# The fourth of four Mamba x halves convolved on VectorE, in a hybrid of convolution, attention, Mamba and a recurrence

## The chip, the cores and the metric

One core of one Trainium2 chip runs the whole program. The metric is the device time of one execution in microseconds (us): the median of several runs. Engines are called by their short names: PE is TensorE, DVE is VectorE, ACT is ScalarE, POOL is GpSimd, SP is the queue that issues most DMAs. PEld is the weight load of PE.

## The reference, cut to what matters

The input x has 4 images of 128 channels and 64 x 64 pixels. Layer 0 is a group norm, three convolutions and a non-local attention. Layer 1 takes the pixels as 4 sequences of 4096 tokens with 128 features, runs a Mamba block forward and one backward over the normalized tokens, adds both, and then runs a recurrence. The change touches the front of the two Mamba blocks alone:

```
zxbcdt = x @ in_proj
z, xbc, dt = jnp.split(zxbcdt, [D_INNER, D_INNER + CONV_DIM], axis=-1)
xp = jnp.pad(xbc, ((0, 0), (K - 1, 0), (0, 0)))
conv = sum((xp[:, i:i + l, :] * conv_w[:, i] for i in range(K))) + conv_b
xbc = jax.nn.silu(conv)
xh, Bm, Cm = jnp.split(xbc, [D_INNER, D_INNER + D_STATE], axis=-1)
...
y = _ssd(xh, dt, A, Bm, Cm) + xh * D[None, None, :, None]
yg = y.reshape(b, l, D_INNER) * jax.nn.silu(z)
```

D_INNER is 256, so xh has two halves of 128 channels in each of two directions: four halves. K is 4: the convolution is causal, along the tokens, with four taps for each channel, and is followed by a Silu. Everything is computed in float32.

## The kernel before, in words

Layer 0 fills the first half of the span, the recurrence the last tenth. Between them, from about 1,697 us on, stands the Mamba stage (function `mamba`). The features lie on the 128 partitions and the tokens run along the free axis. The stage works in **steps** of 128 tokens of each direction and in **groups** of 512 tokens, four steps to a group: 8 groups to a sequence, 32 groups in all. The loop over n (lines 1406 to 1477) takes one step per turn; j = n mod 4 is the step in the group.

A step n does, in this order on PE: `states` (L1212, the chunk's state, into `small`), `turn` for the next step (L1177, transposes of x into `ptr`), `scan` (L1234 and L1242, the outputs y), `prepare` for the next step (L1187 p_bt and L1189 p_g, into `small`). ACT does for a step the differences of decay (`lt`, L1168, eight relus), their exponential (L1191) and a copy of the transposed B (`bt`, L1193). DVE multiplies x with dt (L1196), makes `gm` (L1200), multiplies it into `lt` (L1201), and adds the new state (`S`, L1224).

Spread over the four steps is what prepares the next group and finishes the last:
- step j = 0: x projection (backward, half 0), `project_bc` for B, x projection (forward, half 1)
- step j = 1: means of the last group (L1282), x projection (backward, half 1), `project_bc` for C
- step j = 2: `project_fwd` (forward, half 0), the Silus of the three other halves (`activate`, L1139), four z projections (L1146, L1147)
- step j = 3: the output projections (`back`, L1305)

The x halves are convolved in two ways. `project` (lines 1118 to 1135) takes three of the four: PE makes one projection without taps (L1124), ACT writes bias plus the last tap times the projection (L1129, an Identity), and DVE adds the three other taps, shifted, straight from PSUM (L1135); the first columns are cleared and added from the last group (L1128, L1133). The Silu comes later, in place, in SBUF (L1139). `project_fwd` (lines 1110 to 1116) takes the fourth: the tap is multiplied into the weights beforehand (L970), so PE runs four matmuls of 128x512 that add up in PSUM (L1115), and ACT applies bias and Silu (L1116). B and C use PE's way as well (L1103, L1107).

All these projections, the z projections, the output projections and the transposes of the row statistics of other sequences (`ls_in`, L83, run at the end of a step by the generators `opening` and `ending`) share a ring of three PSUM buffers ("big", pool `m_ring`). A buffer is taken in program order and comes free when its last reader is done.

The order of instructions on PE and on ACT is written out by hand: it is the order of the calls in the loop (`manual_schedule` for these two). DVE, POOL and the DMA queues are ordered by the framework's planner. Each engine takes its instructions in order.

Of the kernel before, what the change touches and what calls it, by code (L numbers as in the profile page):

```python
# [10 lines left out]
F32 = mybir.dt.float32  # L11
AF = mybir.ActivationFunctionType
ALU = mybir.AluOpType
# [3 lines left out]
P = 128  # L17
# [9 lines left out]
DS = 64  # L27
DI = NHEAD * HD
KC = 4
GT = NC // P  # L30
DIRS = ("fwd", "bwd")
MG = 512
# [116 lines left out]
def run(parts):  # L149
    for _ in parts:  # L150
        pass
# [736 lines left out]
def mamba(nc, tc, k, a, t, B, T, vec, first=None, after=None, mr=None):  # L888
# [16 lines left out]
    with ExitStack() as ctx:  # L905
# [24 lines left out]
        wp = ctx.enter_context(tc.tile_pool(name="m_w", bufs=1))  # L930
        w = []
# [5 lines left out]
        with tc.tile_pool(name="m_ws", bufs=1) as ws, tc.tile_pool(name="m_wps", bufs=2, space=PSUM) as wps:  # L937
            full, cw = [], []
            for i, d in enumerate(DIRS):
                full.append(ws.tile([P, 2 * DI + 2 * DS + NHEAD], F32, name="full_" + d))  # L940
                nc.sync.dma_start(full[i], a[d + "_in_proj"])

                at = DI if i else 0
                cw.append(ws.tile([P, KC, DI + 2 * DS - at], F32, name="cw_" + d))
                nc.scalar.dma_start(
                    cw[i], a[d + "_conv_wt"][:, at:].unsqueeze(0).to_broadcast([P, KC, DI + 2 * DS - at])
                )
            if first is not None:
                scales(0, first)
            for i, d in enumerate(DIRS):  # L950
                centre(nc, k, wps, "c", full[i])
                nc.scalar.copy(wdt[:, bass.ts(i, NHEAD)], full[i][:, 2 * DI + 2 * DS :])
            if first is not None:
                run(scaled(0))
            for i, d in enumerate(DIRS):
                s = dict(taps=vec["taps_" + d], cb=vec["cb_" + d], D=vec["D_" + d])
                w.append(s)
                nc.gpsimd.memset(mean[:, i, i : i + 1], 1.0 / DI)
                f = full[i]
                s["z"] = wp.tile([P, DI], F32, name="wz_" + d)  # L960
                s["x"] = wp.tile([P, DI] if i else [P, KC, P], F32, name="wx_" + d)
                s["bc"] = wp.tile([P, KC, 2 * DS], F32, name="wbc_" + d)


                for c in range(KC):
                    nc.vector.tensor_tensor(
                        s["bc"][:, c, :], f[:, 2 * DI : 2 * DI + 2 * DS], cw[i][:, c, -2 * DS :], ALU.mult
                    )
                    if i == 0:
                        nc.gpsimd.tensor_tensor(s["x"][:, c, :], f[:, DI : DI + P], cw[i][:, c, 0:P], ALU.mult)  # L970
                if i:
                    nc.scalar.copy(s["x"], f[:, DI : 2 * DI])
                else:
                    s["x1"] = wp.tile([P, P], F32, name="wx1")
                    nc.scalar.copy(s["x1"], f[:, DI + P : 2 * DI])
                nc.scalar.copy(s["z"], f[:, 0:DI])
            for i, d in enumerate(DIRS):
                out = wp.tile([P, 2, P], F32, name="wout_" + d)
                w[i]["out"] = out
                nc.scalar.dma_start(out, a[d + "_out_proj"].rearrange("(c p) m -> p c m", p=P))  # L980
                for c in range(2):
                    nc.gpsimd.tensor_scalar(out[:, c, :], out[:, c, :], vec["nw_" + d][:, c : c + 1], None, ALU.mult)
# [4 lines left out]
        ring = ctx.enter_context(tc.tile_pool(name="m_ring", bufs=3, space=PSUM))  # L987
# [6 lines left out]
        def rows(g, i, c):  # L994

            return ds(g * MG + c if i == 0 else (NG - 1 - g) * MG + 2 * PAD - c, MG)
# [110 lines left out]
            act = lambda: nc.scalar.activation(gr["bc"][c], pb, AF.Silu, bias=bc_bias[:, c : c + 1])  # L1107
            act() if later is None else later.append(act)

        def project_fwd(gr):  # L1110

            tl, g = gr["tl"], gr["at"][1]
            px = ring.tile([P, MG], F32, tag="big", name="px")
            for tap in range(KC):
                nc.tensor.matmul(px, w[0]["x"][:, tap, :], tl[:, rows(g, 0, tap)], start=(tap == 0), stop=(tap == KC - 1))  # L1115
            nc.scalar.activation(gr["x"][0][:, 0, :], px, AF.Silu, bias=w[0]["cb"][:, 0:1])  # L1116

        def project(gr, i, c):


            tl, g = gr["tl"], gr["at"][1]
            px = ring.tile([P, MG], F32, tag="big", name="px")
            wx = w[1]["x"][:, bass.ts(c, P)] if i else w[0]["x1"]
            nc.tensor.matmul(px, wx, tl[:, rows(g, i, PAD)], start=True, stop=True)  # L1124
            x = gr["x+"][i][:, c, :]
            taps = w[i]["taps"][:, c, :]
            at = lambda n: x[:, PAD - n : PAD - n + MG] if i else x[:, n : n + MG]
            nc.vector.memset(x[:, 0:PAD] if i else x[:, MG:], 0.0)  # L1128
            nc.scalar.activation(at(0), px, AF.Identity, scale=taps[:, PAD:KC], bias=w[i]["cb"][:, c : c + 1])  # L1129
            if g:  # L1130
                v = x[:, MG:] if i else x[:, 0:PAD]
                past = groups[gr["at"][0] * NG + g - 1]["x+"][i][:, c, :]
                nc.vector.tensor_tensor(v, v, past[:, 0:PAD] if i else past[:, MG:], ALU.add)  # L1133
            for n in range(1, KC):
                nc.vector.scalar_tensor_tensor(at(n), px, taps[:, PAD - n : KC - n], at(n), ALU.mult, ALU.add)  # L1135
# [160 lines left out]
                m2.rearrange("q n -> (q n)").unsqueeze(0).to_broadcast([P, ND * MG]),  # L1296
            )

        STEPS_X = ((1, 0), (0, 1), (1, 1))

        def outputs(gr, d):
            po = ring.tile([P, MG], F32, tag="big", name="po")
# [47 lines left out]
        seqs, groups, m = {}, {}, {}  # L1350
# [42 lines left out]
        open_step(1)  # L1393
        for act in later:
            act()
        project_fwd(groups[0])
        for i, c in STEPS_X:
            project(groups[0], i, c)
        differences(m[0])
# [6 lines left out]
        for n in range(N):  # L1406
            G, j = divmod(n, MT)
            b, g = divmod(G, NG)
            gr = groups[G]
            last = g == NG - 1  # L1410
            if n + 2 < N:
                open_step(n + 2)
            if n % NT == 0:
                S = None
            S1 = states(m[n], S)
            if n + 1 < N:
                turn(m[n + 1])
            if n % 2 == 0:
                y = ps.tile([P, ND, 2, 2 * P], F32, tag="y", name="y")
            scan(m.pop(n), y, S)  # L1420
            S = S1
            if n + 1 < N:
                prepare(m[n + 1])
            if n % 2:
                take(gr, j, y)
            more = G + 1 < NGR
            if j == 0:
                if more:
                    open_group(G + 1)
                if G > 0:  # L1430
                    squares(groups[G - 1])
                if more:
                    project(groups[G + 1], *STEPS_X[0])
                if more:
                    project_bc(groups[G + 1], 0)
                if more:
                    project(groups[G + 1], *STEPS_X[1])
            elif j == 1:
                if G > 0:
                    means(groups[G - 1])  # L1440
                if more:
                    project(groups[G + 1], *STEPS_X[2])
                if more:
                    project_bc(groups[G + 1], 1)
            elif j == 2:
                if more:
                    project_fwd(groups[G + 1])
                if more:
                    for i, c in STEPS_X:
                        activate(groups[G + 1], i, c)  # L1450
                for i in range(ND):
                    for c in range(2):
                        project_z(gr, i, c)
                gate(gr, 1)
            elif j == 3:
                gate(gr, 3, not more)
                if not more:
                    squares(gr, (0,))
                if G > 0:
                    back(groups.pop(G - 1))  # L1460
            if n + 2 < N:
                differences(m[n + 2])

            i = n % NT
            if i == 4:
                opening = open_sequence(b + 1) if b + 1 < B else iter(())
            if i >= 4:
                run(islice(opening, 1))
            if i == 5:
                ending = ended(b - 1) if after is not None and b > 0 else iter(())  # L1470
            if i >= 5 and i % 2:
                run(islice(ending, 1))

            if mr is not None and b == B - 1 and i in (24, 25, 28, 29):
                if i == 24:
                    own = row_statistics(nc, k, ring, "big", wk, t[:, b * T :], mr, (3, 4, 2, 5, 1, 6))
                next(own)
# [276 lines left out]
```

## Time and profile before

| | |
|---|---|
| time | 3146.06 us, median of 3 (3143.19 to 3150.89) |
| span of the profiled run | 3144.2 us, granted PE clock 0.981 |
| PE busy | 2939.4 us, 93% |
| DVE busy | 2198.3 us, 70% |
| ACT busy | 1815.3 us, 58% |
| POOL busy | 1799.3 us, 57% |
| L1115, the four taps on PE | 4 matmuls of 128x512 in each of 32 groups, 256 records in the profile |
| L1124, a projection without taps | 3 in each group, 192 records |
| L1135, the multiply-adds on DVE | 288, about 749 ns each |
| L1129 and L1139 on ACT | 96 each, 778 and 619 ns (medians) |
| L1116 on ACT | 32, 687 ns, and 31 table loads of 1283 ns |

The profile writes every float32 matmul as two records of MATMUL, one behind the other; the time of one record is that of a pipelined pass, and the distance from start to start is less than it. In views that list instructions, the bracket at the end of a line tells how long the engine sat idle before it and what it waited for.

### The profile page before, as it was taken

Reading aid. Unit: us, or ns where it says so; the run is one execution under the profiler, and the core shown is the slowest. Engines: PE = TensorE matmul, PEld = TensorE weight load, DVE = VectorE, ACT = ScalarE, POOL = GpSimd, SP = SyncE. Lnnn points to the kernel's source line nnn. Section 1 sums busy time; section 2 is a strip of 40 time slices with the busy share of each in tenths; the row PEclk is TensorE's granted clock in tenths of the full one; section 3 lists DMA queues with packets and bytes.
Section 4 is the critical chain, followed back from the end, with each engine's and each line's share of the span. In section 5 each row is a group of like instructions: output and inputs, shape, how many; then the busy total and the mean of one; then the engine's idle time right before and its main releaser. Section 6 shows DMA issues by size and latency. Waiting matters only on the chain. (4 is left out here: it accounts for less than half of the span.)

```text
span 3144.2 us, 42863 instructions
## 1 busy us (share of the span) xinstructions
PE 2939.4 (93%) x15511; PEld 1459.0 (46%) x15511; DVE 2198.3 (70%) x3429; ACT 1815.3 (58%) x3102; POOL 1799.3 (57%) x1394
## 2 busy tenths in 40 slices
PE   6899999999999999999997999999999999999976
PEld 1345444454444454444453444444444445455545
DVE  7876668666777667687765767677677767676667
ACT  3343334434344433444434878787788778888756
POOL 4258448456584655766553565555555665555644
PEclk9999999999999999999998999999999999999988
DMA  5310101010100101011023333334343344333332
GB/s 182 133 40 29 38 31 45 8 43 23 46 23 30 43 23 38 31 53 34 10 77 93 93 116 93 96 95 113 84 101 92 88 112 97 96 95 98 92 109 109
DMA packets 108394, 224.16 MB, mean 71 GB/s; under 512 B 25678, under 2 KB 29390, under 8 KB 106764
## 3 DMA queue, kind: packets, MB, share of 16 engines
q1 hardware_dynamic: 96588, 177.53, 20.4%
q10 hardware_dynamic: 11584, 43.78, 4.1%
q8 instruction: 125, 2.05, 0.3%
q14 instruction: 97, 0.79, 0.1%
HBM read 200.83 MB, written 20.44 MB: 70 GB/s over the span
## 5 line engine op out<-in xcount | busy, mean ns | idle before, releaser
L477 DVE TENSOR_TENSOR es<-es,ex 128x1024 f32<-128x1024 f32 x448 | 684.2, 1527 | 137.6 <-ACT ex L462 104.5
L462 ACT ACTIVATE ex<-pf 128x1024 f32<-128x1024 f32 x512 | 497.5, 1022 | 462.3 <-PE pf L460 420.2
L460 PE MATMUL pf<-theta,phi 64*128 64x512 f32 x2048 | 513.6, 619 | 20.2 <-ACT ex L462 19.8
L471 PE MATMUL acc<-ex,gT 128*64 128x512 f32 x2048 | 490.8, 605 | 1.6 <-ACT ex L462 1.6
L1202 POOL TENSOR_TENSOR ct<-ct,Cst 128x512 f32<-128x512 f32 x128 | 171.4, 1339 | 403.2 <-DMA ct<-csmem 365.0
L460 PEld LDWEIGHTS pf<-theta,phi 64*128 64x128 f32 x2048 | 173.3, 186 | 339.4 <-ACT ex L462 173.0
L1168 ACT ACTIVATE lt<-lt,cs 128x128 f32<-128x128 f32 x1024 | 312.1, 390 | 0.5 <-DMA lt<-csmem 0.5
L367 PE MATMUL pm<-yf,wt 128*128 128x256 f32 x1152 | 287.1, 382 | 12.2 <-DVE att L483 11.0
L410 ACT ACTIVATE eo<-pm 128x256 f32<-128x256 f32 x88 | 33.8, 384 | 449.5 <-PE pm L367 443.0
L471 PEld LDWEIGHTS acc<-ex,gT 128*64 128x64 f32 x2048 | 127.4, 136 | 338.2 <-issue 326.3
L367 PEld LDWEIGHTS pm<-yf,wt 128*128 128x128 f32 x1152 | 212.9, 189 | 93.7 <-issue 39.0
L1103 PE MATMUL pb<-tl,wbc_fwd 128*64 128x512 f32 x512 | 236.2, 604 | 3.2 <-DVE xT L1135 3.2
L1103 PE MATMUL pb<-tl,wbc_bwd 128*64 128x512 f32 x512 | 236.7, 604 | 0.0
L337 POOL TENSOR_TENSOR yf<-yd 128x272 f32<-128x272 f32 x192 | 234.1, 1247 | 1.4
L1267 POOL TENSOR_TENSOR yT<-yT,zT 128x512 f32<-128x512 f32 x127 | 169.3, 1342 | 35.8 <-DVE yT L1254 32.2
L337 POOL TENSOR_TENSOR yf<-xp 128x272 f32<-128x272 f32 x128 | 109.7, 889 | 133.3 <-PE pm L367 127.5
L1201 DVE TENSOR_TENSOR lt<-lt,gm 128x1024 f32<-128x1024 f32 x128 | 180.1, 1407 | 1.9
L1135 DVE SCALAR_TENSOR_TENSOR xT<-px,taps_bwd,xT 128x512 f32<-128x512 f32 x192 | 143.7, 749 | 8.9 <-ACT xT L1129 4.0
L1234 PE MATMUL y<-lt,xdt 128*64 128x128 f32 x2048 | 142.4, 282 | 4.9 <-PE ptr L1177 4.6
L1103 PEld LDWEIGHTS pb<-tl,wbc_fwd 128*64 128x64 f32 x512 | 65.5, 138 | 164.3 <-issue 137.1
L367 PE MATMUL pm<-yf,wc 128*128 128x256 f32 x512 | 131.5, 385 | 6.6 <-DVE att L483 5.1
L414 DVE SCALAR_TENSOR_TENSOR eo<-pm,eo 128x256 f32<-128x256 f32 x176 | 72.4, 412 | 92.2 <-ACT eo L410 90.1
(297 smaller groups left out, 5694.7 us busy)
## 6 DMA issues: line engine op xcount, KB each, us to landing
lt<-csmem SPq DMA_DIRECT2D x128, 512.0 KB, 5.6
wt<-wd ACTq DMA_DIRECT2D x72, 576.0 KB, 3.8
ct<-csmem SPq DMA_DIRECT2D x256, 128.0 KB, 5.4
rs<-m SPq DMA_DIRECT2D x31, 512.0 KB, 3.9
wd<-t SPq DMA_DIRECT2D x16, 576.0 KB, 2.8
t<-in_x SPq DMA_DIRECT2D x4, 2048.0 KB, 10.8
rows<-after SPq DMA_DIRECT2D x32, 256.0 KB, 5.3
out<-t SPq DMA_DIRECT2D x4, 2048.0 KB, 14.4
```

Of the source, the lines that this page charges most:

```text
L337: nc.gpsimd.tensor_tensor(f[:, kx], at(x), at(y), op)
L367: nc.tensor.matmul(pm[:, e, :], wt, src, start=(i == 0), stop=(i == len(terms) - 1))
L460: nc.tensor.matmul(pf[:, e, :], phi[HALF[e], m, :], th[HALF[e]], start=True, stop=True)
L462: nc.scalar.activation(ex, pf, AF.Exp, scale=scale)
L471: nc.tensor.matmul(acc[HALF[e]], gT[:, 2 * m + e, :], ex[:, e, :], start=(m == 0), stop=(m == NT // 2 - 1))
L477: nc.vector.tensor_tensor(es, es, ex, ALU.add)
L1103: nc.tensor.matmul(out, w[i]["bc"][:, tap, bass.ts(c, DS)], src, start=(tap == 0), stop=(tap == KC - 1),)
L1135: nc.vector.scalar_tensor_tensor(at(n), px, taps[:, PAD - n : KC - n], at(n), ALU.mult, ALU.add)
L1168: nc.scalar.activation(v, v, AF.Relu, scale=-1.0, bias=m["b"]["cs"][:, d, m["i"], h : h + 1])
L1201: nc.vector.tensor_tensor(lt, lt, gm.unsqueeze(2).to_broadcast([P, ND, NHEAD, P]), ALU.mult)
L1202: nc.gpsimd.tensor_tensor(m["ct"], m["ct"], Cs[:, cols].unsqueeze(1).to_broadcast([P, NHEAD, P]), ALU.mult)
L1267: eng.tensor_tensor(v, v, gr["z"][d][:, :, half(d, j // 2)], ALU.mult)
```

## The change

The fourth half goes the way of the three others. `project_fwd` is gone; `project` treats all four (direction, half) pairs alike, and the list of pairs becomes ((1, 0), (0, 1), (1, 1), (0, 0)). The new projection stands at the end of step j = 1, behind `project_bc` for C, and its Silu is the last of now four in-place Silus in step j = 2. The weights multiplied by taps for this half are not made any more (four POOL products), and the broadcast of the taps that they needed gets smaller. The purpose is to take three of the four matmuls of this half off PE.

```diff
-                at = DI if i else 0
-                cw.append(ws.tile([P, KC, DI + 2 * DS - at], F32, name="cw_" + d))
+                cw.append(ws.tile([P, KC, 2 * DS], F32, name="cw_" + d))
...
-                    if i == 0:
-                        nc.gpsimd.tensor_tensor(s["x"][:, c, :], f[:, DI : DI + P], cw[i][:, c, 0:P], ALU.mult)
-                if i:
-                    nc.scalar.copy(s["x"], f[:, DI : 2 * DI])
-                else:
-                    s["x1"] = wp.tile([P, P], F32, name="wx1")
-                    nc.scalar.copy(s["x1"], f[:, DI + P : 2 * DI])
+                nc.scalar.copy(s["x"], f[:, DI : 2 * DI])
...
-        def project_fwd(gr):
-
-            tl, g = gr["tl"], gr["at"][1]
-            px = ring.tile([P, MG], F32, tag="big", name="px")
-            for tap in range(KC):
-                nc.tensor.matmul(px, w[0]["x"][:, tap, :], tl[:, rows(g, 0, tap)], start=(tap == 0), stop=(tap == KC - 1))
-            nc.scalar.activation(gr["x"][0][:, 0, :], px, AF.Silu, bias=w[0]["cb"][:, 0:1])
...
-            wx = w[1]["x"][:, bass.ts(c, P)] if i else w[0]["x1"]
+            wx = w[i]["x"][:, bass.ts(c, P)]
...
-        STEPS_X = ((1, 0), (0, 1), (1, 1))
+        STEPS_X = ((1, 0), (0, 1), (1, 1), (0, 0))
...
-        project_fwd(groups[0])
         for i, c in STEPS_X:
             project(groups[0], i, c)
...
                     project(groups[G + 1], *STEPS_X[2])
                 if more:
                     project_bc(groups[G + 1], 1)
+                if more:
+                    project(groups[G + 1], *STEPS_X[3])
             elif j == 2:
-                if more:
-                    project_fwd(groups[G + 1])
                 if more:
                     for i, c in STEPS_X:
                         activate(groups[G + 1], i, c)
```

More of the change, by code (lines that the diff above doesn't have):

```diff
@@ L941, in mamba @@
                 nc.sync.dma_start(full[i], a[d + "_in_proj"])
-                at = DI if i else 0
-                cw.append(ws.tile([P, KC, DI + 2 * DS - at], F32, name="cw_" + d))
+                cw.append(ws.tile([P, KC, 2 * DS], F32, name="cw_" + d))
                 nc.scalar.dma_start(
-                    cw[i], a[d + "_conv_wt"][:, at:].unsqueeze(0).to_broadcast([P, KC, DI + 2 * DS - at])
+                    cw[i], a[d + "_conv_wt"][:, DI:].unsqueeze(0).to_broadcast([P, KC, 2 * DS])
                 )
@@ L960, in mamba @@
                 s["z"] = wp.tile([P, DI], F32, name="wz_" + d)
-                s["x"] = wp.tile([P, DI] if i else [P, KC, P], F32, name="wx_" + d)
+                s["x"] = wp.tile([P, DI], F32, name="wx_" + d)
                 s["bc"] = wp.tile([P, KC, 2 * DS], F32, name="wbc_" + d)
```

## The prediction

> **What bounds the kernel now.** I read the table of engines first: PE is busy 93% of the span, DVE 70%, ACT 58%. The change acts only from 1,697 us on (the Mamba stage), so next I asked for the busy time from 1,738 to 2,950 us, where all but the first of its groups of 512 tokens open:
>
> ```profile
> 1738.00:2950.00 1212.00, 1158.72 (x7868) 587.93 (x7867) 854.42 (x1866) 973.47 (x1925) 698.30 (x580) 0.99 0.39 98
> ```
>
> The columns after the length are PE, PE weight loads, DVE, ACT, POOL, then the granted clock. PE is busy 96%, but ACT 80% and DVE 70%: PE leads, ACT is close behind. The chain of waits confirms PE for most of a group. A mean does not tell what ACT can take, so I read the timeline of ACT around the edited call, for the group opened at 2,340-2,356 us:
>
> ```profile
> 2344.58 0.69 ACT L1107 ACTIVATE Cst<-pb,bc_bias 128x512 f32<-128x512 f32 x1 [1.51 <-PE pb L1103]
> 2345.16 2.43 ACT L1168 ACTIVATE lt<-lt,cs 128x128 f32<-128x128 f32 x8
> 2347.61 1.28 ACT L1191 ACT_TABLE_LOAD   x1
> 2348.91 1.06 ACT L1191 ACTIVATE lt<-lt 128x1024 f32<-128x1024 f32 x1
> 2349.87 0.25 ACT L1193 COPY bt<-small 128x128 f32<-128x128 f32 x1
> 2350.14 1.28 ACT L1116 ACT_TABLE_LOAD   x1
> 2351.53 0.69 ACT L1116 ACTIVATE xT<-px,cb_fwd 128x512 f32<-128x512 f32 x1
> 2352.12 1.66 ACT L1139 ACTIVATE xT<-xT 128x512 f32<-128x512 f32 x3
> 2353.68 1.56 ACT L1147 ACTIVATE zT<-pz 128x512 f32<-128x512 f32 x3
> ```
>
> The reader is to see that ACT runs with hardly a hole from 2,344.58 to 2,355.2, while PE does as long a piece: its four taps (L1115) end just as the table load does. Two paths of equal length run from the end of the C projection (pb) to the fourth z projection. That fourth pz needs the ring slot of the first pz, which ACT frees:
>
> ```profile
> 2354.31 1.13 PE L1146 MATMUL pz<-tl,wz_bwd 128*128 128x512 f32 x2 [0.24 <-ACT zT L1147]
> ```
>
> How equal they are in each group is read from the source view of L1116, how long ACT waited for the taps:
>
> ```profile
>   PE px L1115: 30.4, 22
> ```
>
> Group by group (31 calls in the loop) the time between the end of the table load and the Silu is 0.1 us nine times, 0.34 once, 0.85 eight times, 1.2 four times, 2.06 nine times. Only where it is large is PE the longer path.
>
> **What the Trainium skill says.** "ScalarE: Activation LUTs", "What ACT_TABLE_LOAD costs" and "Table sets": a load takes 1283 ns, and identity and relu are in every set. The trace agrees: all loads are 1283 ns, and L1129 (Identity) has none. "TensorE: Matmul & The Clock Gate", Part 2, step 1: matmuls stay in program order. The trace agrees: at 2,354 us PE waits for the slot although the transposes behind it (L1177) follow at once. The same page, Part 1: after an idle window of about 3.4 us the PE clock falls to half until about 3.4 us of activity. The trace agrees on the half rate and puts the threshold lower: of PE's seven idle gaps over 2 us in the stage, five (4.22 twice, 2.86, 2.37, 2.13) are followed by slow matmuls (a px pair takes 2.07 instead of 1.13), two (2.76, 2.53) are not, and none of the gaps of 0.8-1.2 us is. After the 2.86 gap the stretch from pcs to the scan's second half takes 6.36 us, after the 2.37 gap 5.07, after the undisturbed 2.76 gap 3.50: a drop costs 1.6 to 2.9 us.
>
> **The change, part by part.**
> *PE.* Four taps of a 128x512 projection become one. They stand as 8 records at 0.43 us, 3.65 us in the chain of waits; a single projection (L1124) takes 1.06. PE alone saves 2.59 us a group, but at two places: 3.65 leave step 2, 1.06 come into step 1, right behind the C projection.
> *ACT.* Step 1 gains an Identity (L1129, 0.78 us). The same pattern stands in step 0 of this trace: Silu of B at 2,333.59, Identity of the projection behind it at 2,334.65, relu at 2,335.32, so 1.73 us from Silu to relu. In step 1 now it is 0.58. **ACT's path gets 1.15 us longer.** In step 2 a fourth in-place Silu (0.52 us from start to start) replaces one from PSUM (0.58): -0.06. The table load moves to the first in-place Silu; no load more or less.
> *DVE.* Three more multiply-adds of 0.749 us (L1135), a memset and an add of 3 columns: 2.6 us a group, 32 x 2.6 = 83 us busy. In the changed program's order on DVE they stand behind xdt and xdtd where there are no row statistics, in the 2.2-2.8 us hole in which DVE waits for ACT's bt copy: free. Where row statistics (L85) run in step 1 they stand ahead of the state update S (L1224), and PE's next p_bt (L1187) waits for S.
> *POOL, DMA, setup.* Four products of weights (L970, 4 x 0.65 us) and 512 KB of broadcast go. POOL then waits for wout's DMA anyway (2.68 us at L982), and cw has long landed: nothing.
> *Who waits.* The fourth pz is queued behind three pz on PE, and behind it all of turn, scan, po. So the time of that pz is what counts. Its shift, by class:
> - 0.1 us (9 groups): ACT is the path. 1.15 - 0.06 - 0.1 = +1.0; nine make +9.0. The one of 0.34: +0.75.
> - 0.85 (8, one row statistic): +0.24 each, +1.9. S comes about 1 us late, but the bt copy has 1.2 us of room on PE's side.
> - 1.2 (4): three -0.1; in the fourth (2,232 us) DVE lags, the slot that the row statistic takes is freed 2.3 us later: +0.9. Sum +0.6.
> - 2.06 (9): four with two row statistics: p_bt waits for S, which comes after 3 multiply-adds and 8 statistics: bt +1.4, then no wait: -0.65 each. Two with one: -0.8. Three with pcs in step 1: the new px waits for ms (L1284), bt comes 1-1.8 us later: -0.8. Sum -6.6.
> The opening group, where DVE is the chain (4.71 us of L1135 and others before the Silu): three more at 0.67, start 0.7 sooner: +1.4.
> **Sum of the paths: +7 us.**
> *The clock.* This is the unknown. PE now runs ahead and waits before the fourth pz. In the 0.1 groups: step 2 begins for PE at 2,347.8 + 1.0, three pz end at 2,351.5, the fourth starts at 2,355.3: a gap of 3.8 us instead of 0.24. In the 0.85 groups it is 2.0, in three of the 1.2 groups 2.7, in two of the 2.06 groups 2.1, else about 1.6. By the seven gaps above I take a drop as certain at 3.5 and more (10 groups), 0.7 at 2.7 and 0.5 at 2.0-2.1 (10 groups), none below. At 1.6 us, the low end since part of the slow time falls into the gap: 16 + 3.4 + 8 = 27. Bounds: 0 (no drop matters), and 31 x 2.1 = 65.
> I take the paths plus the middle of the clock's cost: 3146 + 7 + 27 = 3180, given as 3179.
>
> **The rivals.**
> 1. *PE is the bound and keeps its gain.* For it: 93% busy, PE on most of the chain. 32 x 2.59 = 83 us would give 3063; if only the groups' PE path with ACT's floor counts and ACT hides its Identity, about 1.0-1.5 a group, so 3100-3115. Against: nine groups with no wait at the Silu, where a shorter PE frees nothing. I take 3108. Faster.
> 2. *A draw.* The paths as above and no clock cost: 3153. For it: two gaps of 2.5-2.8 us passed undisturbed.
> 3. *DVE becomes the bound.* The 2.6 us fall on the state update in every group: 31 x 2.6 = 81 would give 3227; in the 17 groups with statistics or pcs, 44 us, plus the sum of the paths, 3197. For it: PE waits for S already (L1187, 34 us in 2,000-2,720). Against: DVE idles about 6 us in step 2.
>
> **How the numbers follow.** Forecast (ACT path, clock) 0.50; draw 0.25; PE's gain 0.12; DVE 0.13. Faster by over 0.3% (below 3136.6) is rival 1: 0.12. Within 0.3% (to 3155.5): 0.15 of the draw and 0.03 of the forecast: 0.18. Slower: 0.70. The range, 3141 to 3214, leaves out rival 1 and the upper part of rival 3.
>
> **What would show it.** Right: PE's wait for ACT before pz (6.8 us between 1,750 and 2,900 us now) at about 75 us; the granted clock of the stage under 0.99; relu of step 1 1.73 us after the Silu of C; ACT busy +23 us (32 x (0.78 + 0.62 - 0.69)); DVE +80; steps 2 followed by slow scans in the 0.1 groups. Wrong: if the fourth pz starts sooner than before in the 0.1 groups, or if waits for S at L1187 grow far over 60 us (rival 3), or if the gaps stand there and the scans behind them stay at 1.09 us (rival 2).

## The result, and the profile after

The changed kernel takes 3196.82 us (median; 3188.05 to 3199.23, 4 runs) against 3147.31 us (3143.19 to 3150.89; 4 runs, one more than in the table of before). The ratio is 1.0153, with a 95% interval of 1.013 to 1.0176: 1.5% slower, and 18 us above the forecast of 3179. PE does less work, and the program is longer. First, the engines of the changed kernel, from the first part of its page:

```profile
PE 2884.2 (91%) x15319; PEld 1429.8 (45%) x15319; DVE 2278.5 (72%) x3585; ACT 1838.7 (58%) x3134; POOL 1797.2 (56%) x1390
```

Against before, PE lost 55.2 us of busy time (2939.4), DVE gained 80.2 (2198.3) and ACT 23.4 (1815.3); POOL is all but unchanged. The span of this execution is 3186.0 us against 3144.2. The same stretch of the Mamba stage as in the prediction, from the view of windows (columns as there):

```profile
1738.00:2950.00 1212.00, 1075.82 (x7432) 544.35 (x7430) 898.34 (x1947) 964.30 (x1891) 673.19 (x561) 0.97 0.39 95
```

PE fell from 1158.72 to 1075.82 us of 1212, and its granted clock from 0.99 to 0.97. So PE idles and runs slower when it works. Lines move by the lines taken out: L1116 is gone, L1129 (Identity) is now L1113, the multiply-adds L1119, in-place Silu L1123, pz L1130, zT L1131, p_bt L1171, S L1208. ACT's timeline in the same group as in the prediction, one of the 0.1 class (in which ACT waited only 0.1 us for the taps):

```profile
2365.61 0.69 ACT L1099 ACTIVATE Cst<-pb,bc_bias 128x512 f32<-128x512 f32 x1 [1.51 <-PE pb L1095]
2366.67 0.78 ACT L1113 ACTIVATE xT<-px,cb_fwd,taps_fwd 128x512 f32<-128x512 f32 x1 [0.37 <-PE px L1108]
2367.35 2.44 ACT L1152 ACTIVATE lt<-lt,cs 128x128 f32<-128x128 f32 x8
2369.80 1.28 ACT L1175 ACT_TABLE_LOAD   x1
2371.09 1.06 ACT L1175 ACTIVATE lt<-lt 128x1024 f32<-128x1024 f32 x1
2372.06 0.25 ACT L1177 COPY bt<-small 128x128 f32<-128x128 f32 x1
2372.32 1.28 ACT L1123 ACT_TABLE_LOAD   x1
2373.62 2.19 ACT L1123 ACTIVATE xT<-xT 128x512 f32<-128x512 f32 x4
2375.71 1.55 ACT L1131 ACTIVATE zT<-pz 128x512 f32<-128x512 f32 x3
```

The relus start 1.74 us behind the Silu of C (2,367.35 less 2,365.61) where it was 0.58, and from there ACT has no hole up to zT. PE's timeline of the same group shows what that does, first the two lines behind the fourth pz before the change, then the changed kernel:

```profile
2355.28 0.60 PE L1177 MATMUL ptr<-ident,xT 128*128 128x128 f32 x4
2355.81 1.09 PE L1234 MATMUL y<-lt,xdt 128*64 128x128 f32 x16
```

```profile
2370.03 1.99 PE L1130 MATMUL pz<-tl,wz_fwd 128*128 128x512 f32 x4
2371.86 1.02 PE L1130 MATMUL pz<-tl,wz_bwd 128*128 128x512 f32 x2
2376.34 1.68 PE L1130 MATMUL pz<-tl,wz_bwd 128*128 128x512 f32 x2 [3.46 <-ACT zT L1131]
2377.82 1.06 PE L1161 MATMUL ptr<-ident,xT 128*128 128x128 f32 x4
2378.80 1.75 PE L1218 MATMUL y<-lt,xdt 128*64 128x128 f32 x16
```

Three pz are done early, the fourth waits 3.46 us for the buffer that ACT frees (0.24 before), and then the clock is low: the pz takes 1.68 instead of 1.13, the transposes 1.06 instead of 0.60, the scan 1.75 instead of 1.09. The view of waits (us in total, times, longest) adds the same wait over the stage, and a second one. The first two lines are of before, from 1,750 to 2,900 us, the last two of the changed kernel, from 1,750 to 2,940 us; both stretches hold 28 fourth pz:

```profile
PE pz L1146 <- ACT zT L1147: 6.8, 28, 0.2
PE small L1187 <- DVE S L1224: 19.6, 19, 4.2
```

```profile
PE pz L1130 <- ACT zT L1131: 65.7, 28, 3.5
PE small L1171 <- DVE S L1208: 42.8, 35, 5.9
```

The wait ahead of the fourth pz grew from 6.8 to 65.7 us; the other, PE's p_bt waiting for the state that DVE adds, from 19.6 to 42.8.

I then split the 30 periods between the first and the last of the 31 fourth pz (of the groups that still prepare a next one; from start to start) into time in which PE records run and time between them (worked out from the two timelines of PE):

| from fourth pz of the first group to that of the last | length, us | PE busy | PE idle |
|---|---|---|---|
| before | 1211.0 | 1157.7 | 53.3 |
| after | 1251.9 | 1111.4 | 140.5 |

The projection takes 30 x 2.59 = 77.7 us of work off PE. Busy time fell by 46.3 only, so the rest of the work got 31.4 us slower; idle time grew by 87.3. The sum is +40.9 us of this execution's 41.8.

### The profile page after: what moved, and what is told of

It is laid out like the page before. It is cut to its first block, busy times and chain, and to the rows that moved or that the text cites. A ratio compares the mean times of both kernels' runs of the same rounds, so it can differ in the third digit from the quotient of the medians.

```text
span 3186.0 us, 42657 instructions
## 1 busy us (share of the span) xinstructions
PE 2884.2 (91%) x15319; PEld 1429.8 (45%) x15319; DVE 2278.5 (72%) x3585; ACT 1838.7 (58%) x3134; POOL 1797.2 (56%) x1390
## 4 chain that ended last, share of the span: by engine, by line
PE 67%; DVE 13%; ACT 8%; POOL 5%; issue 3%; DMA 3%; SPq 0%; ACTq 0%; POOLq 0%; DVEq 0%
PE acc L471 13%; PE pf L460 13%; PE pm L367 13%; PE pb L1095 5%; PE px L1108 3%; PE y L1218 2%; PE acc L1559 2%; DVE att L483 2%; DVE xT L1119 2%; PE po L1289 2%; ACT lt L1152 1%; PE pm L1266 1%; PE pz L1130 1%; ACT xT L1123 1%; PE ptr L1161 1%
## 5 line engine op out<-in xcount | busy, mean ns | idle before, releaser
L1119 DVE SCALAR_TENSOR_TENSOR xT<-px,taps_bwd,xT 128x512 f32<-128x512 f32 x192 | 144.1, 750 | 9.2 <-ACT xT L1113 3.4
L1205 POOL TENSOR_TENSOR S<-S,tot 128x256 f32<-128x256 f32 x120 | 92.5, 771 | 94.3 <-PE y L1226 75.5
L1119 DVE SCALAR_TENSOR_TENSOR xT<-px,taps_fwd,xT 128x512 f32<-128x512 f32 x192 | 142.2, 741 | 2.5 <-ACT xT L1113 0.5
L1130 PE MATMUL pz<-tl,wz_bwd 128*128 128x512 f32 x128 | 74.3, 664 | 74.8 <-ACT zT L1131 73.8
```

## The experiments

My theory: ACT's path, not PE's, sets the fourth pz (it got longer by its Identity), so PE's gain becomes idle time, and this idle time costs again through the clock. The rivals: DVE has become the bound; or PE's gain is real and is lost elsewhere. Where a table below gives busy and idle, it is the split just described.

**1. Work put into the gap.** The third pz, which ends just ahead of the gap, is run three times (the second and third write the same values again).

```diff
-            nc.tensor.matmul(pz, w[i]["z"][:, bass.ts(c, P)], ...)
+            for _ in range(3 if (i, c) == (1, 0) else 1):
+                nc.tensor.matmul(pz, w[i]["z"][:, bass.ts(c, P)], ...)
```

> The changed kernel, in which PE runs the third z projection (backward, half 0) three times into the same buffer: 2 x 0.86 us more PE work in every group, put into the gap before the fourth z projection, nothing else changed. Theory (ACT's path plus the clock): in the traces PE's busy time between the fourth z projection of a group and the Silu of C of the next grew by 25 us on the same work, which I take for the clock. With the gaps cut from 3.46 to about 1.7, from 2.05 to 0.3 and from 2.55 to 0.8 us the drops should vanish: 3197 - 20 to - 25, so about 3175, granted clock of the stage back at 0.98 to 0.99, and the path part (+7) and the other waits (+10) unchanged. Rival (the clock is not what costs; PE's gap is only idle time): not faster than 3197, and up to a few us slower where the gap was only 1.6 us.

Measured: 3171.68 us, ratio 1.0079 (1.0059 to 1.0099), 25 us faster than the changed kernel, with some 53 us more of work for PE (31 x 1.72; the backward pair takes 2.74 us below for three matmuls where it took 1.02 for one). PE's timeline of the same group (lines are one further down in this kernel):

```profile
2366.09 2.74 PE L1131 MATMUL pz<-tl,wz_bwd 128*128 128x512 f32 x6
2370.57 1.13 PE L1131 MATMUL pz<-tl,wz_bwd 128*128 128x512 f32 x2 [1.74 <-ACT zT L1132]
2371.54 0.60 PE L1162 MATMUL ptr<-ident,xT 128*128 128x128 f32 x4
2372.07 1.10 PE L1219 MATMUL y<-lt,xdt 128*64 128x128 f32 x16
```

The gap is 1.74 us, and pz, transposes and scan run at full rate. Counted from the Silu of C, the fourth pz starts within 0.15 us of its place in the changed kernel in 26 of the 31 groups: there the added matmuls cost nothing, so PE is not the bound. (Of the five others four start 1.2 to 2.5 us later and one 0.9 sooner, together +6.) From the start of the fourth pz to the next Silu of C, the same work took 22.3 us less of PE's busy time. This shows the clock's part, and that it comes from the gap.

**2. The other end: fewer taps, nothing for ACT or DVE.** The kernel before with the last tap alone in `project_fwd`, so that PE loses the same time and the other engines gain nothing. Three taps of the forward half 0 are left out of the computation.

```diff
-            for tap in range(KC):
-                nc.tensor.matmul(px, w[0]["x"][:, tap, :], tl[:, rows(g, 0, tap)], start=(tap == 0), stop=(tap == KC - 1))
+            nc.tensor.matmul(px, w[0]["x"][:, PAD, :], tl[:, rows(g, 0, PAD)], start=True, stop=True)
```

> The kernel before, in which the forward half 0 gets its last tap only: three of the four matmuls of L1115 left out, ACT and DVE untouched (the three other taps of this half are not computed). It is PE's part of the change alone, without ACT's and DVE's price. Theory: the fourth z projection can come earlier only by what ACT waited for the taps: 9 x 0.1 + 0.34 + 8 x 0.85 + 4 x 1.2 + 9 x 2.06 = 31 us less, and the gaps that open on PE (about 2.6 us in the nine groups without a wait, 1.9 in the eight of 0.85) give back some 8 to 12 us by the clock: about 3127, range 3115 to 3140. Rival (PE alone is the bound): 32 x 2.59 = 83 us less, 3064.

Measured: 3139.18 us, ratio 0.998 (0.9972 to 0.9987). Of some 80 us of PE work, 7.6 come out in the time. In its split the length is 1203.6 us, busy 1102.1, idle 101.5: 77.7 us less work makes 55.6 less busy time (22.1 come back as slower work) and 48.2 more idle. The fourth pz starts 30.1 us sooner behind the Silu of C, summed over the 31 groups, where I had worked out 31. It gained less than I had expected (3127) since all that follows, from this start to the next Silu of C, got longer by 22.7 us (15.9 busy, 6.7 idle) and not by 8 to 12. So even at no cost to ACT or DVE, PE's gain in this arrangement is worth a tenth of its size.

**3. No work added to DVE.** The changed kernel without DVE's three multiply-adds of the new half; three taps of it are left out of the computation.

```diff
-            for n in range(1, KC):
+            for n in range(1, KC if (i, c) != (0, 0) else 1):
```

> The changed kernel without the three multiply-adds on DVE for the fourth half (its three shifted taps are not computed): 2.25 us a group off DVE, PE and ACT untouched. Theory: DVE only matters through the state update S that PE's p_bt waits for (and through buffers that come free sooner), of which the idle part of +10 us in the traces is the bound: 3197 - 5 to - 12, about 3188. Rival (DVE became the bound): 44 to 81 us less, 3116 to 3153.

Measured: 3200.98 us, ratio 1.0175 (1.0158 to 1.0192): no faster than the changed kernel. That throws out DVE's added work as the bound. It also missed my own 3188. The waits of p_bt for S did shrink, from 42.8 to 26.2 us, but the wait ahead of the fourth pz grew (same view and window, this kernel):

```profile
PE pz L1130 <- ACT zT L1131: 80.8, 28, 3.5
PE small L1171 <- DVE S L1208: 26.2, 26, 4.9
```

In the split it has 1128.6 us busy, 17 more than the changed kernel, for the same work on PE, and 137.5 idle: 18 gaps of 3 us and more where the changed kernel has 12. The longer gaps and slower work took what the shorter waits for S had given. Summed over the split's groups from both timelines, those waits went where they lay between the Silu of C and the fourth zT (15.7 us in the changed kernel, none here); behind it 26.7 us are left of 28.5, so the adds alone do not make them.

**4. C out of ACT's way.** The changed kernel with `project_bc` for C moved from step 1 to the start of step 2, and its Silu behind the four in-place Silus. A group then needs one load of Silu's table and one of Exp's less.

```diff
             elif j == 1:
...
-                    project_bc(groups[G + 1], 1)
...
             elif j == 2:
                 if more:
+                    later = []
+                    project_bc(groups[G + 1], 1, later)
                     for i, c in STEPS_X:
                         activate(groups[G + 1], i, c)
+                    for act in later:
+                        act()
```

> The changed kernel with the projection of C moved from step 1 to the start of step 2, its Silu behind the four in-place Silus: step 1 has no Silu any more, so ACT saves one load of the Silu table and one of the Exp table (2 x 1.28 us) a group and is ahead of PE; PE has 3.6 us of work while ACT does the in-place Silus, so no gap. Theory: with ACT's path out of the way and no clock loss PE keeps the 2.59 - 1.06 = 1.53 us a group that the change takes off it: 3147 - 47 = 3100, range 3085 to 3125. Rival (DVE is the bound, or the gain of PE is lost elsewhere): 3150 or more.

Measured: 3181.54 us, ratio 1.0109 (1.0087 to 1.0131), a miss by 80 us. The periods tell where. From fourth pz to fourth pz, a group without row statistics took 34.82 us (at 2,411 us; before 37.84, changed kernel 40.06): the expected gain is there. Groups with row statistics in step 1 took up to 5 us more than before (48.26 against 43.15 in the one that ends at 2,161 us). PE's timeline in one of these:

```profile
2100.14 1.12 PE L83 MATMUL ls_in<-ident,t 128*128 128x128 f32 x4 [2.84 <-DVE xT L1119]
2101.18 1.12 PE L1196 MATMUL small<-xdtd,bt 128*64 128x256 f32 x4
2102.24 1.12 PE L1161 MATMUL ptr<-ident,xT 128*128 128x128 f32 x4
2103.28 1.96 PE L1218 MATMUL y<-lt,xdt 128*64 128x128 f32 x16
```

The second row statistic of the step needs a buffer of the ring, and with C gone two projections stand side by side in step 1, each of which holds its buffer until DVE has made three multiply-adds. PE waits 2.84 us (3.87 in the next such group), and all that follows is at half rate: 1.12 for transposes that take 0.66. This wait is only a part of it. The view of waits, from 1,750 to 2,940 us, has 14.7 us for `ls_in` behind DVE's multiply-adds, and more for the state:

```profile
PE small L1171 <- DVE S L1208: 53.7, 29, 4.5
```

That is 11 us above the changed kernel. Why S came later here was not tested.

**5. The same move in the kernel before.** C to step 2, with the four taps still on PE; C's projection first, then `project_fwd`.

```diff
             elif j == 2:
                 if more:
-                    project_fwd(groups[G + 1])
+                    later = []
+                    project_bc(groups[G + 1], 1, later)
...
+                    for act in later:
+                        act()
+                    project_fwd(groups[G + 1])
```

> The kernel before (four taps on PE) with the C projection moved from step 1 to the start of step 2, ahead of the taps; its Silu behind the three in-place Silus. ACT loses one load of Silu's table and one of Exp's in each group (2.57 us) and step 1 has no Silu any more. Theory (two equal paths, the taps' is PE's): with the taps still on PE, relieving ACT alone frees only the few tenths that PE waits, so 3140 us (3125 to 3152) against 3147. Rival (ACT alone is the bound in front of the fourth pz, so that PE's taps cost nothing): the 2.57 us come out of most groups, 3075 to 3100.

Measured: 3185.99 us, ratio 1.0128 (1.011 to 1.0146). That relieving ACT alone brings nothing is as expected: in ACT's timeline the Silu of the taps now waits for PE (at 2,375 us):

```profile
2375.05 0.69 ACT L1116 ACTIVATE xT<-px,cb_fwd 128x512 f32<-128x512 f32 x1 [2.94 <-PE px L1115]
```

That it lost 40 us I had not expected. Plain groups take 38.05 us (before 36.7 to 37.8), those that open a sequence 47.3 to 47.6 (42.4 to 45.3): step 1 has lost the 3.6 us of PE work for C that covered DVE's part of the step. PE now waits there for DVE, with one gap of 5.97 us per sequence opened. A kernel with the taps ahead of C on PE was not run.

**6. The fourth projection alone to step 2.** The changed kernel with its new projection at the start of step 2 and the fourth Silu ahead of the last z projection.

```diff
-                if more:
-                    project(groups[G + 1], *STEPS_X[3])
             elif j == 2:
                 if more:
+                    project(groups[G + 1], *STEPS_X[3])
...
-                    for i, c in STEPS_X:
+                    for i, c in STEPS_X[:3]:
...
                     for c in range(2):
+                        if more and i and c:
+                            activate(groups[G + 1], *STEPS_X[3])
                         project_z(gr, i, c)
```

> The changed kernel with the projection of the fourth half moved from the end of step 1 to the start of step 2; three in-place Silus, then zT 0 to 2, then the fourth Silu ahead of the last z projection. Theory (the 1.15 us of Identity in front of the relus of step 1 is what lengthens ACT's path): relu stands 0.58 us behind the Silu of C again, the fourth pz comes some 0.9 us earlier than in the changed kernel in the groups where PE has no slack, and the PE gap ahead of it is split into one of about 2.4 us ahead of the third pz (it needs the buffer that DVE frees) and less than 1 us ahead of the fourth; fewer clock drops. 3163 us (3150 to 3175). Rival (the position of the Identity does not matter, the loss is DVE's extra work or PE's gaps as such): as the changed kernel, 3190 to 3200.

Measured: 3189.66 us, ratio 1.0139 (1.0119 to 1.0158), at the rival's value. The same kind of group on PE:

```profile
2371.13 1.88 PE L1130 MATMUL pz<-tl,wz_fwd 128*128 128x512 f32 x4
2376.50 3.45 PE L1130 MATMUL pz<-tl,wz_bwd 128*128 128x512 f32 x4 [3.49 <-DVE xT L1119]
```

The gap went from ahead of the fourth pz to ahead of the third and is as long as it was: DVE's three multiply-adds stand behind `gm` and `lt` of the step, so the buffer comes free at about 2,376.5, not the 2,375.4 that my 2.4 us of gap meant. The position of the Identity is not tested by this run, since a new wait took the old one's place.

**7. The Identity behind the relus.** PE's order as in the changed kernel; ACT's Identity of the new half, with DVE's adds, behind the eight relus of step 1.

```diff
+            def rest():
                 nc.scalar.activation(at(0), px, AF.Identity, ...)
...
+            rest() if later is None else later.append(rest)
...
+            if j == 1:
+                for act in late:
+                    act()
```

> The changed kernel with ACT's Identity of the fourth half (and DVE's adds to it) placed behind the eight relus of step 1 instead of ahead of them; PE's order unchanged. Theory: ACT no longer waits for px (0.37 us) ahead of the relus, so its path to Exp and to the fourth pz is about 0.4 us shorter in the some 18 groups where ACT sets it, -8 us, and the gap of 3.46 us ahead of the fourth pz becomes 3.0, which spares a few drops of the clock: 3183 us (3172 to 3192) against 3197. Rival (the Identity itself, 0.78 us, counts wherever it stands and the drop of the clock does not depend on 0.4 us): 3190 to 3200.

Measured: 3163.44 us, ratio 1.0069 (1.0044 to 1.0094): 33 us faster than the changed kernel, where I had expected 14. The fourth pz (two lines further down in this kernel):

```profile
2360.64 1.13 PE L1132 MATMUL pz<-tl,wz_bwd 128*128 128x512 f32 x2 [2.98 <-ACT zT L1133]
```

Counted from the Silu of C, the fourth pz starts 0.47 to 0.49 us sooner in 23 of the 31 groups, 1.05 in three, in sum 15.3 us (expected 8); up to the fourth zT the sum over all is -12.2 us. The rest came behind it: -9.8 us of slow work and -7.9 of idle. Here PE's waits for S are 21.2 us from 1,738 to 2,950 us against 42.8 in the changed kernel. Those between the Silu of C and the fourth zT (15.7) are gone, as in experiment 3, which has no adds; those behind it fell from 28.5 to 21.3, which leaving out the adds did not do (26.7). So the later place of DVE's adds is not shown to explain this last part; its cause stays open.

**8. Both to step 2.** The changed kernel with the fourth projection and then C's at the start of step 2. C's work on PE stands between the new projection and the z projections that need its buffer. (The timeline shows 3.6 us for it, from 2,341.37 to 2,344.97, not the 4.3 of my expectations.)

```diff
-                if more:
-                    project_bc(groups[G + 1], 1)
-                if more:
-                    project(groups[G + 1], *STEPS_X[3])
             elif j == 2:
                 if more:
...
+                    later = []
+                    project(groups[G + 1], *STEPS_X[3])
+                    project_bc(groups[G + 1], 1, later)
+                    for i, c in STEPS_X[:3]:
                         activate(groups[G + 1], i, c)
+                    for act in later:
+                        act()
...
+                        if more and i and c:
+                            activate(groups[G + 1], *STEPS_X[3])
                         project_z(gr, i, c)
```

> The changed kernel with both moved to the start of step 2: the projection of the fourth half first, then the C projection (4.3 us on PE), then the z projections; on ACT the Identity, three in-place Silus, Silu of C, zT 0 to 2, fourth Silu, last zT. Two table loads fewer in each group. In the run with C alone moved, the groups without row statistics took 34.8 us from fourth pz to fourth pz (before 36.7 to 37.8, changed kernel 38.6 to 39.9), but those with row statistics in step 1 took 2 to 5 us more than before: there the statistics' transposes needed a buffer of the ring that two projections side by side hold until DVE's six multiply-adds are done, and PE idled 2.8 to 3.9 us. Theory (it was the ring): with one projection in step 1 this wait is gone, PE keeps most of its 2.6 us a group, 3100 us (3075 to 3125), faster than both. Rival (statistics groups lose because DVE has too much work in step 1 and the clock drops): about as with C alone, 3160 to 3185.

Measured: 3116.55 us, ratio 0.9905 (0.9886 to 0.9924): faster than both, by 1% and 2.5%, within the theory's range (3100, 3075 to 3125) and outside the rival's. The z projections on PE, in a plain group:

```profile
2344.97 2.02 PE L1130 MATMUL pz<-tl,wz_fwd 128*128 128x512 f32 x4
2346.83 1.88 PE L1130 MATMUL pz<-tl,wz_bwd 128*128 128x512 f32 x4
2349.11 0.66 PE L1161 MATMUL ptr<-ident,xT 128*128 128x128 f32 x4 [0.41 <-ACT xT L1123]
2349.70 1.09 PE L1218 MATMUL y<-lt,xdt 128*64 128x128 f32 x16
```

No pz waits, the clock is full, and a plain group takes 35.14 us. Experiment 5 has C at the same place and four taps where this one has a projection and DVE's adds: it is the same change again in another arrangement, apart from the order of these two on PE and the place of the fourth Silu on ACT.

| | four taps on PE | one projection, DVE adds |
|---|---|---|
| C in step 1 | 3147 (before) | 3197 (after) |
| C in step 2 | 3186 (5) | 3117 (8) |
| split, C in step 2: length, busy, idle | 1249.3, 1160.0, 89.4 | 1182.4, 1093.9, 88.5 |

With C in step 1 the change costs 50 us, with C in step 2 it brings 69. In the lower row PE's busy time falls by 66.1 us of the 77.7, and its idle time does not grow. How much of the 69 us is due to the different orders is not shown. The new half stands in step 1 in the changed kernel and in step 2 here; experiments 4 and 6 show that both moves are needed.

**9. C back in step 1 where a sequence opens.** The last kernel keeps a gap of 5.97 us per opening. In these groups alone C stays in step 1.

```diff
+                    if n % NT in (25,):
+                        project_bc(groups[G + 1], 1)
...
-                    project_bc(groups[G + 1], 1, later)
+                    if (n - 1) % NT not in (25,):
+                        project_bc(groups[G + 1], 1, later)
```

> The kernel with both projections in step 2 (3116.6 us), except that in the three groups that open the next sequence (step 25 of 32) the C projection stays in step 1, ahead of the cumulative sums pcs. There PE idled 5.97 us ahead of pcs (L1054) for DVE's xe, and the clock fell behind it; with C's 4.3 us in that place the gap should be about 1.7 us and the matmuls behind it at full rate. Theory: these three groups take about 43 us instead of 45.7 (as in the run with the fourth projection alone in step 2), -8 us: 3109 us (3102 to 3115). Rival (the time until xe is DVE's and ACT's alone, and the 2.6 us that ACT gains on these groups are lost again): 3114 to 3124.

Measured: 3115.42 us (3109.78 to 3118.18), ratio 0.9886 (0.9867 to 0.9905), which can't be told from experiment 8 and lies in the rival's range (3114 to 3124), just outside the theory's. The place itself, first in experiment 8 and then here:

```profile
2297.34 0.79 PE L1054 MATMUL pcs<-xe,tri 128*128 128x128 f32 x2 [5.97 <-DVE xe L1041]
```

```profile
2296.59 0.49 PE L1054 MATMUL pcs<-xe,tri 128*128 128x128 f32 x2 [2.37 <-DVE xe L1041]
```

The three groups took 42.84, 41.42 and 41.92 us instead of 45.62, 45.75 and 45.97, together 11 us less, more than the 8 expected, at full rate behind the gap here. The gap is shorter by the 3.6 us of C. But five other groups of the profiled execution (near 1,790, 1,830, 2,150, 2,460 and 2,735 us), which the edit does not touch, took 1.4 to 3.4 us longer, and two (near 1,910 and 2,190 us) 3.3 and 1.7 less. So what pcs waits for is read rightly; a gain of the whole is not shown.

## Why the prediction was right, point by point

- **Two equal paths, ACT's decides: right.** The relus stand 1.74 us behind C's Silu (1.73 predicted), ACT's busy time rose 23.4 us (23), DVE's 80.2 (80), PE's wait for ACT ahead of the pz went from 6.8 to 65.7 us (75). Experiments 1 and 8 show the path from both sides: in 26 of 31 groups work added to PE there costs nothing, and with ACT relieved PE's gain appears. Experiment 2 confirms the reading it rests on: PE's saving brought the fourth pz forward by what ACT had waited for the taps (30.1 us, 31 worked out).
- **The shifts by class: right where ACT is the path.** From the Silu of C to the start of the fourth pz, which is what the prediction worked out, and to the end of its zT, summed over each class:

| class of ACT's wait before, us | groups | predicted | to the pz's start | to the end of zT |
|---|---|---|---|---|
| 0.1 | 9 | +9.0 | +8.9 | +12.6 |
| 0.34 | 1 | +0.75 | +0.75 | +0.75 |
| 0.85 | 8 | +1.9 | +2.1 | +2.4 |
| 1.2 | 4 | +0.6 | -0.5 | +0.1 |
| 2.06 | 9 | -6.6 | -9.7 | -8.9 |

  In the 0.1 class every one of the nine groups shifts by 0.98 or 0.99 us (predicted 1.0). In the 2.06 class the groups lie between -3.5 and +0.03, so there only the sum is near. The path's sum is +1.5 against +5.7 (the opening apart: +0.5 where +1.4 was predicted). Up to the end of zT it is +6.9; these 5.4 us more are the fourth pz itself at a low clock.
- **The gaps: right with small misses.** 3.46 us in eight of the 0.1 class, predicted as 3.8 (the ninth, in the first group, has 2.15); 2.04 to 2.14 in seven of the 0.85 class (2.0); 2.55 and 2.10 (2.7 and 2.1); 3.08 in the class of 0.34, which was counted among those of 3.5 and more; 1.57 to 1.69 for the rest (1.6).
- **The clock: right, with the price taken as it was.** Slow matmuls follow seven of the eight gaps of 3.46 us. On the same work, from the start of the fourth pz to the next Silu of C, PE was busy 30.5 us longer than before (27 predicted). Experiment 1 takes 22.3 of it back.
- **The step that was mis-sized: the state update.** I had written that S comes late in the statistics groups but finds room in the bt copy. PE's wait for S grew by 23 us. Some 15 of these lie ahead of the fourth zT, where the shifts above hold them already; but behind it PE idled 9.8 us more in sum than before, 8.6 of it in waits for S, and nothing in the sum stood for that. These 28.5 us of waits are 29.4 in experiment 1, without slow matmuls behind the gap, and 26.7 in experiment 3, without the adds, so neither alone makes them. With paths 1.5, the opening 0.5, slow work 30.5 and this 9.8 the sum is 42 us, that of the profiled execution. The medians differ by 49.5; the other 8 us are in no trace. The forecast of 33 came as near as it did partly by luck: the paths were put 5 us too high, the clock and the state 13 too low.
- **A reading that was wrong.** The 34 us of waiting for S in the prediction add the weight load's wait (19.0) and the matmul's (15.2), which are the same idle time seen twice. Counted so, the stage went from 45.6 to 95.3 us, past the sign of 60 that the prediction gave for rival 3; the matmuls alone stand at 42.8.
- **The rivals.** A draw falls with the slow scans behind the gaps. DVE as the bound has the measured number among its own (3197) and, by the last count, its sign; it falls with experiment 3, in which DVE's added multiply-adds are left out and nothing is won. PE's gain was wrong for this arrangement and right for another: experiment 8 has 66 us of it.

What stays open: why the clock drops behind some gaps and not behind others of the same length, why PE waits longer for S behind the fourth zT, and which part of experiment 7's gain is DVE's order.

## What to carry to other kernels

Ahead of taking work off the busiest engine, read how long the next engine waited for it at the place where the two meet, group by group: that wait was the most that came out there (experiment 2), and a saving beyond it became idle time. When a second path is as long, shorten it in the same edit (here two table loads, by moving one Silu next to others), and look which buffer each moved projection then holds, since a wait for a slow reader easily takes the place of the one removed. On PE, count idle time of some 2 us and more just ahead of dense work at more than its length, also when it is cut into two gaps (below).

## What the runs showed of the hardware

Repeating a matmul in an idle gap made the program 25 us faster (experiment 1). The prediction quoted "TensorE: Matmul & The Clock Gate" of the Trainium skill, Part 1, with about 3.4 us of idleness; these runs put drops lower, and not at one length. In the changed kernel seven of eight gaps of 3.46 us ahead of the fourth pz were followed by half rate (transposes of 0.66 us took 1.06 to 1.12, or the scan's 1.09 up to 1.98), of three of 2.55 us two, of nine between 2.04 and 2.14 us three; one of 3.08 us and the nine of 1.57 to 1.69 us were not. A gap of 1.74 us was harmless in all seven groups of experiment 1 that have it. But two short gaps can do it: in experiment 2, with 1.54 and 0.92 us of idleness and one pz of 1.13 us between them, six of nine groups were followed by slow matmuls, and in experiment 7 one of four with 0.52 and 1.32 us. So the length of the last gap alone does not decide.
